# Row norms inverted as a 128x4 tile, masked logits in one combined pass with two exponentials, and a new issue order

## The chip, the cores and the metric

The kernel runs on one core of one Trainium2 chip, in float32. The metric is device microseconds of one execution, and lower is better. The time before is 2535.09 us, the median of three runs (2533.92 to 2537.39).

A core has TensorE (PE, matrix products and transposes), VectorE (DVE), ScalarE (ACT), GpSimd (POOL) and SyncE (SP). In this kernel SP issues nearly all DMAs, in one queue. PE writes its results to PSUM; all else lives in SBUF, 128 partitions wide.

## The reference

The input x has 32 batches of 512 tokens with 256 features, and one 512 x 512 adjacency (a 64th of it set) serves all batches. Per batch:

```python
def gat(inp, adj, W, a):                    # graph attention
    h = inp @ W
    f1, f2 = h @ a[:F, 0], h @ a[F:, 0]     # one number per token each
    e = leaky_relu(f1[:, None] + f2[None, :], 0.2)
    if adj is not None:
        e = where(adj > 0, e, -9e15)
    return elu(softmax(e, axis=-1) @ h)

y = layernorm(x)
o0 = relu(y @ mlp1_w + mlp1_b)                       # 512 x 512
o1 = elu(gat(o0, None, W_fc, a_fc)) + o0
o2 = relu(o1 @ mlp2_w + mlp2_b)                      # 512 x 256
x = x + relu(elu(gat(o2, adj, W_hand, a_hand)) + o2)

z = layernorm(x)                                     # slice attention, 8 heads of 64
fx, xm = z @ W_fx + b_fx, z @ W_x + b_x
w = softmax((xm @ W_slice + b_slice) / temp)         # token x 64 slices, per head
norm = w.sum(tokens)                                 # 8 heads x 64 slices = 512 numbers
tok = (w.T @ fx) / (norm + 1e-5)                     # 64 slice tokens per head
q, k, v = tok @ W_q, tok @ W_k, tok @ W_v
out = softmax(q @ k.T / 8) @ v
x = x + (w @ out) @ W_out + b_out
```

## The kernel before, in words

**Recording and issue order.** The program doesn't issue its instructions as it goes through the batches. A `Recorder` (line 52) records every operation of all 32 batches under its batch and under a step name: load, norm1, mlp1, h, factors, p, pv, o1, mlp2, h2, e, p2, pv2, norm2, w, sums, s1T, tokens, att, vo, gg, out. Then `order` (line 251) runs a list scheduler, `_schedule` (line 163), over them: it keeps a modelled time per engine, takes the operation that can start first, and among those that could start, the one with the smallest key. The key is the batch's number times a period plus the step's turn (`TURNS`, line 17; `PERIOD`, 23). A first pass over batches 1 to 12 measures the period, and the second pass takes each step's turn from where that step began in batch 8, with shifts by hand for the first three batches (`HEAD`) and the last three (`TAIL`). Costs of operations come from `_cost` (line 128) and the constants beside it: `SWITCH` is what PE loses between matmuls on different parts of the array, and `ISSUE, BEGIN, LAND, BEHIND` describe DMAs. At most four batches are interleaved. Finally `emit` (line 286) issues everything in that fixed order. So each engine has one fixed queue for the whole run, semaphores hold it to the data, and a change of a modelled cost can move every instruction of every engine. Nearly every instruction carries line 288, where `emit` issues it.

**The steps around the change.** In the middle batches (all but the first and the last) five big transposes and one small one go by DMA: DVE flips blocks of 32 x 32 into a staging tile (`flip`), four DMAs, one for each 32 partitions, write it to DRAM (`scr`), and one DMA reads it back transposed (`gather`). The tiles are xn_stage (first layernorm's result, read back as xnT for mlp1), u_stage (o1T), e_stage (p2T, the masked attention's weights for pv2), o2_stage (r2), xn2_stage (xn_raw, copied to xn2T for the weff products) and w_stage (w_raw, copied to wT for the out step). The first and the last batch transpose on PE, except o2.

- *norm1, mlp1*: DVE makes xn; xnT times w1 gives o0T on PE.
- *h*: o0T times W_fc in seven products of halves (Strassen and Winograd's way); DVE sums the left operands into `mix`.
- *pv, o1, mlp2, h2*: the attention without mask needs no 512 x 512 logits: its weights pT are built from vectors of 512. PE then does pT times h, the second layer and o2 times W_hand, with f1 and f2 as extra columns.
- *e*: four tiles of 128 rows. For each, DVE makes the logits (f2 from PSUM, f1 per row, `mbias` the mask as a large negative number), the leaky relu and the negated row maximum, ACT the exponential with that maximum as bias, and DVE the flip:

```python
nc.vector.scalar_tensor_tensor(
    e, f2b, h[:, i, D : D + 1], mbias[:, i, :], op0=OP.add, op1=OP.add)
nc.vector.scalar_tensor_tensor(e, e, ALPHA, e, op0=OP.mult, op1=OP.max)
nc.vector.tensor_reduce(nmax[:, i : i + 1], e, axis=AX.X, op=OP.max, negate=True)
nc.scalar.activation(e, e, AF.Exp, bias=nmax[:, i : i + 1])
```

- *norm2, w*: the second layernorm; xn2T times weff (W_x and W_slice in one) on PE, and its softmax over 64 slices per head on DVE and ACT.
- *sums*: xn times w, summed over tokens, into s1T (128 x 2 x 512). The last row of xn is 1, so s1T's last row holds the 512 norms.
- *s1T*: SP copies that one row to DRAM (`line`), and two DMAs spread it over the partitions of `rn` (128 x 256), where DVE adds 1e-5 and takes the reciprocal.
- *tokens, att, vo, gg*: W_fx times s1T (PE), times rn (DVE) is tok; then wqk times tok gives q, q times tok the scores, a softmax (sc, on DVE and ACT), its transposes and products with tokT (mean), and wvo to gg, one after another and each small.
- *out*: gg times wT on PE, added to x on DVE, and the store.

Of the kernel before, what the change touches and what calls it, by code (L numbers as in the profile page):

```python
# [10 lines left out]
AF = mybir.ActivationFunctionType  # L11
OP = mybir.AluOpType
AX = mybir.AxisListType
# [1 line left out]
ENGINES = ("tensor", "vector", "scalar", "gpsimd", "sync")  # L15

TURNS = {
    "load": -462.5, "norm1": 57.6, "mlp1": 1478.5, "h": 1624.1, "factors": 1626.7, "p": 1631.1,
    "pv": 1644.1, "o1": 1647, "mlp2": 1694.9, "h2": 1709.3, "e": 1714.6, "p2": 1102.3,
    "pv2": 1733.3, "norm2": 1780.6, "w": 1806.7, "sums": 1812.1, "s1T": 1826.8, "tokens": 2321.2,  # L20
    "att": 658.3, "vo": 1004.5, "gg": 1394.8, "out": 1524.2,
}
PERIOD, SPARE = 89.9, 0.01

HEAD = (
    (-33, 108, 3, -726, 0, 63, -4, 93, -317, -118, -101, -31, 114, 36, 581, -77, -43, -443, 55,
     -1, 16, -659),
    (302, 200, 0, 41, 0, 223, 198, 0, -15, 0, 760, -14, -1674, -151, 33, -31, -61, -1067, 191,
     -140, -300, 8),
    (-6, 37, 1179, -81, 0, 0, -1864, -1, 0, 1, -105, -68, -395, 94, 4, -151, 5, 3, -336, 3, 0,  # L30
     0),
)
TAIL = (
    (-203, -62, 1108, 0, -19, -60, 101, 4, -242, -90, -82, 1, -58, -418, -434, 1119, -43, -15,
     -10, 0, -198, 0),
    (295, 0, 75, 221, 12, 158, -7, 50, -1, 64, 0, 173, -8, -61, -5, 0, 30, 0, -59, -299, 730,
     197),
    (94, 1079, -126, 0, -154, 915, -18, 0, 0, -1924, -62, -58, -41, 72, -15, 360, 0, -238, 0,
     -132, -14, 140),
)  # L40


# [3 lines left out]

P = 128
ALPHA = 0.2
MASKED = -4.5e16


class Recorder:
# [3 lines left out]
    SIGNAL = 0.06  # L56
    DRAIN = 0.17
    ISSUE, BEGIN, LAND, BEHIND = 0.45, 2.2, 0.0, 3.6
    SWITCH = 0.1
    KEPT = 1  # L60
    AHEAD = 3

# [65 lines left out]
    def _cost(self, op, out, ins):  # L128


        def words(ap):
            return ap.size() // ap.ap[0][1]

        n = words(out)
        if op.method == "dma_start":
            side = next(ap for ap in (out, *ins) if ap.space != bass.MemoryType.DRAM)
            kb = out.size() / 256
            if side.ap[0][1] <= P // 4:
                op.moving = 0.3 + max(0.0, 1.08 * (kb / 128 - 1))
            else:  # L140
                op.moving = max(1.5 * kb / 512, 4.0 * kb / 1024 - 0.5)
            return self.ISSUE, 0.0
        if op.engine == "tensor":
            one = max(n / 1200 + 0.002, 0.109)
            if op.mode == (P, P // 2):
                one = max(n / 2400, 0.0275)
            elif op.mode == (P // 2, P // 2):
                one = max(n / 4800, 0.0135)
            return (one if op.method == "transpose" else 2 * one), self.DRAIN
        if op.engine == "scalar":  # L150
            pointers = sum(isinstance(op.kwargs.get(k), bass.AP) for k in ("bias", "scale"))
            return 0.06 + n / 1200 + 0.09 * pointers + 0.19 * ("accum_out" in op.kwargs), 0.12
        if op.engine == "vector":
            n = max([n] + [words(x) for x in ins])
            single = op.method in ("tensor_copy", "tensor_scalar")
            fast = single and all(x.space != bass.MemoryType.PSUM for x in ins)
            pointers = sum(words(x) == 1 for x in ins) if n > 1 else 0
            return 0.07 + n / (1920 if fast else 960) + 0.065 * pointers, 0.1
        if n < 16:
            return (0.1 if op.method == "memset" else 0.3 if op.method == "tensor_scalar" else 1.1), 0.1  # L160
        return 0.2 + n / (480 if op.method == "tensor_tensor" else 960), 0.1

    def _schedule(self, ops, key, spare):
# [35 lines left out]
        while len(done) < len(ops):  # L199
# [21 lines left out]
            if op.engine == "tensor" and op.mode != mode:  # L221
                t, mode = t + self.SWITCH, op.mode
            op.start, op.end = t, t + op.cost + op.lag
# [102 lines left out]
def adj_ffn_kernel(  # L326
# [26 lines left out]
    B, N, D = x.shape  # L353
    HID = mlp1_w.shape[1]
    HH = HID // 2
    NT = N // P
    KD = D // P
# [5 lines left out]
    NP = INNER // P  # L363
    assert G == C == 64 and HEADS * G == 512 and N == 512 and HID == 512 and D == 256

    nc = Recorder(tc.nc)
# [5 lines left out]
    def ts(i, n=P):  # L372
        return slice(i * n, (i + 1) * n)

    def new(name, shape, bufs=1, tag=None, dtype=F32):
        return sbuf.tile(list(shape), dtype, name=name, tag=tag or name, bufs=bufs)

    def mm_tile(shape):
        return psum.tile(shape, F32, tag="bank", name="mm", bufs=8)

    def tr_tile(shape):
        return psum.tile(shape, F32, tag="bank", name="tr", bufs=8)
# [7 lines left out]
    def flip(src, dst):  # L390

        nc.vector.transpose(dst, src.rearrange("p (c i) -> p c i", i=Q))

    def by_dma(what, b):

        return what in FLIPPED and b not in EDGES
# [19 lines left out]
    def med(name, shape=(P, 4, 256)):  # L416
        return new(name, shape, bufs=2, tag="med")

    def row(name, shape=(P, 512), tag=None):
        return new(name, shape, bufs=2, tag=tag)  # L420

    def small(name, shape):
        return new(name, shape, bufs=3)
# [8 lines left out]
    def load_x(b):  # L432
# [14 lines left out]
        out=ident, in_=ident, compare_op=OP.not_equal, fill=1.0, base=0,  # L447
# [75 lines left out]
    mbias = new("mbias", [P, NT, N], dtype=BF16)  # L523
# [10 lines left out]
    for t in range(NT):  # L534
# [4 lines left out]
        nc.vector.tensor_scalar(  # L539
            mbias[:, t, :], mbias[:, t, :], -1.0, -MASKED, op0=OP.add, op1=OP.mult  # L540
        )
# [69 lines left out]
    for p in range(NP):  # L611
        pv = mm_tile([P, D])
# [49 lines left out]
    def front(b):  # L662
# [20 lines left out]

        h = new("h", [P, NT, 2, HH + 1])
        l11, l12, l21, l22 = (o0T[:, ts(k, 2), ts(t, 2 * P)] for t in range(2) for k in range(2))
        mix = new("mix", [P, 4, 2, 2 * P])
        s1, s2, s3, s4 = (mix[:, i] for i in range(4))
        for to, left, op, right in (
            (s1, l21, OP.add, l22), (s2, s1, OP.subtract, l11),
# [32 lines left out]
        f1, f2 = h[:, :, 0, HH], h[:, :, 1, HH]  # L722
# [30 lines left out]
        pT = new("pT", [P, NT, N])  # L753
        for j in range(NT):
# [5 lines left out]
                op0=OP.mult, op1=OP.max,  # L760
# [6 lines left out]
        for i in range(NT):  # L767
# [9 lines left out]
            u, m = row("u"), row("m")  # L777
# [13 lines left out]
        if by_dma("u", b):  # L791
            gather("u", stage, o1T)
            for m in range(KH):
                o1 = o1T[:, m, :].rearrange("p (t a i) -> p t a i", t=NT, i=Q)
# [3 lines left out]
    def middle(b, o1T):  # L798
# [12 lines left out]
        h = new("h2", [P, NT, D + 2], tag="h" if b == B - 1 else None)  # L811
# [7 lines left out]
        f2b = tr_tile([P, N])  # L819
        for j in range(NT):  # L820
            nc.tensor.transpose(f2b[:, ts(j)], h[:, j, D + 1 : D + 2].to_broadcast([P, P]), ident)
        if not by_dma("e", b):
            pt, f2b = f2b, new("f2b", [P, N], tag="acb")
            nc.scalar.copy(f2b, pt)
        nc.step = "e"
        pT = new("p2T", [P, NT, N], tag="pT" if b == B - 1 else None)
        if by_dma("e", b):
            stage = new("e_stage", [P, N // Q, P], bufs=2, tag="stage")
        nmax = small("nmax", [P, NT])
        for i in range(NT):  # L830
            e = new("e", [P, N], bufs=2)
            nc.vector.scalar_tensor_tensor(
                e, f2b, h[:, i, D : D + 1], mbias[:, i, :], op0=OP.add, op1=OP.add
            )
            nc.vector.scalar_tensor_tensor(e, e, ALPHA, e, op0=OP.mult, op1=OP.max)
            nc.vector.tensor_reduce(
                nmax[:, i : i + 1], e, axis=AX.X, op=OP.max, negate=True
            )
            nc.scalar.activation(e, e, AF.Exp, bias=nmax[:, i : i + 1])
            if by_dma("e", b):  # L840
                flip(e, stage[:, :, ts(i, Q)])
                continue
            pt = tr_tile([P, NT, P])
            for j in range(NT):
                nc.tensor.transpose(pt[:, j, :], e[:, ts(j)], ident)
            nc.scalar.copy(
                pT.rearrange("p j (t a i) -> p j t a i", t=NT, i=Q)[:, :, :, i, :],
                pt.rearrange("p j (t i) -> p j t i", i=Q),
            )
# [18 lines left out]
        for i2 in range(NT // 2):  # L868
            parts = []
            for s in range(2):  # L870
                i = 2 * i2 + s
# [8 lines left out]
            u, m = row("u2", (P, 2, D), "u"), row("m2", (P, 2, D), "m")  # L880
# [10 lines left out]
    def back(b, x1):  # L891
# [17 lines left out]
        w = new("w", [P, NT, INNER], tag="o0T" if b == B - 1 else None, bufs=1 + (b == B - 1))  # L909
# [34 lines left out]
        s1T = med("s1T", (P, KD, INNER))  # L944
# [8 lines left out]
        if by_dma("w", b):  # L953
            raw = new("w_raw", [P, NP, N], tag="w")
            gather("w", stage_w, raw)
            for p in range(NP):
                nc.scalar.copy(
                    wT[:, p, :].rearrange("p (t a i) -> p t a i", t=NT, i=Q), swapped(raw[:, p, :])
                )
        nc.step = "s1T"  # L960
        line = dram.tile([NP, 2, G], F32, name="line", tag="line", bufs=2)
        nc.sync.dma_start(
            line.rearrange("(o p) s g -> o (p s g)", o=1), s1T[P - 1 : P, KD - 1, :]
        )
        rn = new("rn", [P, NP, G], tag="mean")
        for s in range(2):
            nc.sync.dma_start(
# [3 lines left out]
                    ap=[[0, C], [2 * G, NP], [1, G]],  # L971
                ),
            )
        nc.vector.tensor_scalar(rn, rn, 1e-5, None, op0=OP.add)
        nc.vector.reciprocal(rn, rn)
        nc.step = "tokens"

        nc.joint = True
# [17 lines left out]
        q = new("q", [P, 2, 2, G])  # L996
# [57 lines left out]
        gg = med("gg")  # L1054
# [33 lines left out]
    for b in range(B):  # L1088
        nc.age = b
        back(b, middle(b, front(b)))  # L1090
# [57 lines left out]
```

## Time and profile before

| | before |
|---|---|
| median of 3 runs | 2535.09 us (2533.92 to 2537.39) |
| the profiled execution, its own time | 2531.39 us |
| its span in the profile | 2529.6 us |
| mean granted TensorE clock | 0.996 |
| PE busy, matmuls | 2487.6 us |
| DVE busy | 2157.7 us |
| ACT busy | 1059.7 us |
| DMA moved | 348.60 MB |

The profiler recorded one execution. Its own time is 1.8 us longer than the span, and 3.7 us shorter than the median. Busy time is the sum over an engine's instructions, each from start to end. Matmuls overlap, so one starts before the other ends, and their mean durations are longer than the pitch at which they start. The chain of work that ended last is followed back from the last instruction, at each step to what released it. In lists of instructions, a line reads: line of the code, engine, operation, output<-inputs by the program's names, shapes, count; idle time before, with what ended it, stands in brackets or behind the last bar.

### The profile page before, as it was taken

To read this page: it belongs to the slowest core of one execution; us is meant where nothing else is said; L and a number is where in the kernel's file an instruction comes from. 1 tells how busy PE (TensorE), PEld (TensorE's weight loads), DVE (VectorE), ACT (ScalarE), POOL (GpSimd) and SP (SyncE) were. 2 spreads that over 40 slices of the span, in tenths; PEclk is the share of its full clock that TensorE was granted. 3 is DMA by queue.
4 is the path that set the end of the run, shared out by engine and by line. 5 is a ranking of instruction groups with operands and counts; after the bars stand their busy time and mean duration, and the time that the engine had idled before them with its cause. 6 is when DMAs were issued, how large, how long until landed. Compare 5 with 4: busy or idle time off the path is not lost.

```text
span 2529.6 us, 33819 instructions
## 1 busy us (share of the span) xinstructions
PE 2487.6 (98%) x11653; PEld 1726.1 (68%) x11653; DVE 2157.7 (85%) x5108; ACT 1059.7 (42%) x1941; POOL 101.1 (4%) x167
## 2 busy tenths in 40 slices
PE   7999999999999999999999999999999999999988
PEld 5767667776667666677666676766676666767655
DVE  7778889988889888889888898888898888888865
ACT  3434343433444434444434434334444344444432
POOL 0000000000000000000000000000000000000000
PEclk9999999999999999999999999999999999999989
DMA  5243456544556544555544565445565445545432
GB/s 162 59 120 94 130 155 169 158 128 127 136 160 170 148 126 131 151 160 160 135 132 128 160 172 148 131 134 136 160 169 144 127 130 155 162 127 148 109 97 63
DMA packets 441985, 348.60 MB, mean 138 GB/s; under 512 B 101044, under 2 KB 366388, under 8 KB 441814
## 3 DMA queue, kind: packets, MB, share of 16 engines
q1 hardware_dynamic: 440230, 345.39, 50.3%
q8 instruction: 93, 1.52, 0.2%
q10 hardware_dynamic: 1584, 1.05, 0.1%
q14 instruction: 78, 0.64, 0.1%
HBM read 186.92 MB, written 159.45 MB: 137 GB/s over the span
## 4 chain that ended last, share of the span: by engine, by line
PE 81%; ACT 6%; DVE 6%; DMA 5%; SPq 1%; issue 1%; POOL 0%; DVEq 0%; ACTq 0%
PE mm L288 79%; ACT pT L288 2%; PE tr L288 2%; DMA rn<-line 2%; ACT acb L288 2%; SPq L288 1%; DMA xn_raw<-scr 1%; ACT o2T L288 1%; DVE rn L288 1%; DVE acb L288 1%; DMA scr<-xn_stage 1%; DVE u L288 1%; DVE h L288 1%; DVE xn_stage L288 1%; DVE xn L288 0%
## 5 line engine op out<-in xcount | busy, mean ns | idle before, releaser
L288 PEld LDWEIGHTS mm<-h,pT 128*128 128x128 f32 x2048 | 385.8, 189 | 152.0 <-issue 87.9
L288 PE MATMUL mm<-h,pT 128*128 128x257 f32 (+1 forms) x2048 | 483.8, 379 | 1.6 <-DVE pT L288 1.6
L288 PE MATMUL mm<-weff,xn2T 128*128 128x512 f32 x512 | 256.3, 607 | 1.7 <-ACT xn2T L288 1.7
L288 PE MATMUL mm<-w,xn 128*128 128x512 f32 x512 | 252.8, 592 | 0.0
L288 PE MATMUL mm<-o1T,w 128*128 128x512 f32 x512 | 246.8, 593 | 0.8 <-DVE o1T L288 0.8
L288 PE MATMUL mm<-xnT,w 128*128 128x512 f32 x512 | 232.3, 603 | 0.7 <-ACT xnT L288 0.7
L288 PE MATMUL mm<-gg,wT 128*128 128x256 f32 x1024 | 230.5, 379 | 0.8 <-DVE gg L288 0.8
L288 PE MATMUL mm<-h,p2T 128*128 128x257 f32 x1024 | 228.2, 380 | 0.0
L288 PEld LDWEIGHTS mm<-gg,wT 128*128 128x128 f32 x1024 | 193.6, 190 | 41.0 <-issue 15.0
L288 ACT ACTIVATE e<-e,nmax 128x512 f32<-128x512 f32 x128 | 92.4, 722 | 294.9 <-DVE nmax L288 294.8
L288 PEld LDWEIGHTS mm<-h,p2T 128*128 128x128 f32 x1024 | 194.0, 190 | 29.4 <-issue 1.2
L288 DVE TENSOR_TENSOR h<-mm,h 128x257 f32<-128x257 f32 x320 | 128.8, 419 | 61.7 <-PE mm L288 61.0
L288 PEld LDWEIGHTS mm<-xnT,w 128*128 128x128 f32 x512 | 95.1, 191 | 107.9 <-issue 102.5
L288 ACT ACTIVATE m<-m 128x512 f32<-128x512 f32 x192 | 120.9, 630 | 112.2 <-DVE m L288 112.2
L288 ACT COPY h<-mm 128x258 f32<-128x258 f32 (+1 forms) x256 | 95.0, 373 | 135.9 <-PE mm L288 135.3
L288 ACT ACTIVATE u<-mm,rd 128x256 f32<-128x256 f32 x192 | 90.3, 470 | 145.0 <-DVE rd L288 68.4
L288 ACT ACTIVATE w<-w 128x512 f32<-128x512 f32 x128 | 80.7, 630 | 162.4 <-DVE w L288 162.2
L288 DVE SCALAR_TENSOR_TENSOR pT<-acb,ex,pT 128x512 f32<-128x512 f32 x128 | 94.0, 745 | 63.8 <-ACT pT L288 63.8
L288 ACT ACTIVATE m<-m,neg 128x512 f32<-128x512 f32 x192 | 138.4, 721 | 5.3
L288 DVE SCALAR_TENSOR_TENSOR u<-m,u 128x512 f32<-128x512 f32 x192 | 129.7, 675 | 11.7 <-ACT m L288 11.5
L288 ACT COPY xn2T<-xn_raw 128x512 f32<-128x512 f32 x60 | 34.2, 615 | 245.9 <-DMA xn_raw<-scr 245.9
L288 PEld LDWEIGHTS mm<-o1T,w 128*128 128x128 f32 x512 | 91.6, 189 | 58.0 <-issue 39.5
(150 smaller groups left out, 4208.8 us busy)
## 6 DMA issues: line engine op xcount, KB each, us to landing
scr<-xn_stage SPq DMA_DIRECT2D x240, 128.0 KB, 2.5
scr<-u_stage SPq DMA_DIRECT2D x120, 256.0 KB, 5.9
o1T<-scr SPq DMA_DIRECT2D x30, 1024.0 KB
scr<-e_stage SPq DMA_DIRECT2D x120, 256.0 KB, 4.9
p2T<-scr SPq DMA_DIRECT2D x30, 1024.0 KB, 5.5
scr<-w_stage SPq DMA_DIRECT2D x120, 256.0 KB, 4.8
w_raw<-scr SPq DMA_DIRECT2D x30, 1024.0 KB, 7.9
x<-in_x_dram SPq DMA_DIRECT2D x32, 512.0 KB
```

The lines of the kernel that those rows point to most:

```text
L288: getattr(getattr(self.nc, op.engine), op.method)(*op.args, **op.kwargs)
```

## The change

- The planner: all of `TURNS`, `PERIOD`, `HEAD` and `TAIL` are new; `SWITCH` goes from 0.1 to 0.17, the modelled cost of a 64 x 64 matmul up by a fifth, and `reciprocal` gets a cost of its own.
- `mix` shares the buffer of `pT`.
- e: one `tensor_tensor_reduce` per tile adds f2 and the mask and takes the row maximum (`top`) in the same instruction; the profile's program has it as two, the pass and a read of its 128x1 result. f1, being one number per row, is added to the four maxima at once (128 x 4), which then go through the leaky relu. The leaky relu of the logits is left to ACT: exp of a maximum is the maximum of exponentials, so ACT takes one exponential with f1 - top as bias and one of 0.2 times the logit, and DVE takes the larger. Four tiles e are held instead of two, since all four maxima come before the first exponential. `MASKED` is a power of two.
- s1T: the norms' row goes by DMA into a tile of 128 x 4 (`norm`), is inverted there, goes to DRAM and is then spread; `rn` arrives inverted. That is one DMA per batch more.

```diff
@@ TURNS, PERIOD, HEAD, TAIL: all numbers
-    "load": -462.5, "norm1": 57.6, "mlp1": 1478.5, "h": 1624.1, "factors": 1626.7, "p": 1631.1,
...
-PERIOD, SPARE = 89.9, 0.01
+    "load": 361.5, "norm1": -64.6, "mlp1": 945.4, "h": 1108, "factors": 1115.3, "p": 1133,
...
+PERIOD, SPARE = 89.08, 0.01
...
-MASKED = -4.5e16
+MASKED = -(2.0 ** 55)
...
-    SWITCH = 0.1
+    SWITCH = 0.17
...
-                one = max(n / 4800, 0.0135)
+                one = max(n / 4000, 0.0135)
...
+            if op.method == "reciprocal":
+                return 0.05 + n / 145, 0.1
...
-        mix = new("mix", [P, 4, 2, 2 * P])
+        mix = new("mix", [P, 4, 2, 2 * P], tag="pT")
...
-        nmax = small("nmax", [P, NT])
-        for i in range(NT):
-            e = new("e", [P, N], bufs=2)
-            nc.vector.scalar_tensor_tensor(
-                e, f2b, h[:, i, D : D + 1], mbias[:, i, :], op0=OP.add, op1=OP.add
-            )
-            nc.vector.scalar_tensor_tensor(e, e, ALPHA, e, op0=OP.mult, op1=OP.max)
-            nc.vector.tensor_reduce(
-                nmax[:, i : i + 1], e, axis=AX.X, op=OP.max, negate=True
-            )
-            nc.scalar.activation(e, e, AF.Exp, bias=nmax[:, i : i + 1])
+        f1, top, low = h[:, :, D], small("top", [P, NT]), small("low", [P, NT])
+        masked = [new("e", [P, N], bufs=4) for i in range(NT)]
+        for i, e in enumerate(masked):
+            nc.vector.tensor_tensor_reduce(
+                out=e, in0=f2b, in1=mbias[:, i, :], scale=1.0, scalar=3.0 * MASKED,
+                op0=OP.add, op1=OP.max, accum_out=top[:, i : i + 1],
+            )
+        nc.vector.tensor_tensor(top, top, f1, op=OP.add)
+        nc.vector.scalar_tensor_tensor(top, top, ALPHA, top, op0=OP.mult, op1=OP.max)
+        nc.vector.scalar_tensor_tensor(low, f1, ALPHA, top, op0=OP.mult, op1=OP.subtract)
+        nc.vector.tensor_tensor(top, f1, top, op=OP.subtract)
+        for i, e in enumerate(masked):
+            above = row("above", tag="m")
+            nc.scalar.activation(above, e, AF.Exp, bias=top[:, i : i + 1])
+            nc.scalar.activation(e, e, AF.Exp, scale=ALPHA, bias=low[:, i : i + 1])
+            nc.vector.tensor_tensor(e, e, above, op=OP.max)
             if by_dma("e", b):
                 flip(e, stage[:, :, ts(i, Q)])
...
         nc.step = "s1T"
+        norm = new("norm", [P, NP], bufs=2)
+        nc.sync.dma_start(norm, s1T[P - 1 : P, KD - 1, :])
+        nc.vector.tensor_scalar(norm, norm, 1e-5, None, op0=OP.add)
+        nc.vector.reciprocal(norm, norm)
         line = dram.tile([NP, 2, G], F32, name="line", tag="line", bufs=2)
-        nc.sync.dma_start(
-            line.rearrange("(o p) s g -> o (p s g)", o=1), s1T[P - 1 : P, KD - 1, :]
-        )
+        nc.sync.dma_start(line.rearrange("p s (q f) -> (p s q) f", f=NP), norm)
         rn = new("rn", [P, NP, G], tag="mean")
...
-        nc.vector.tensor_scalar(rn, rn, 1e-5, None, op0=OP.add)
-        nc.vector.reciprocal(rn, rn)
```

## The prediction

> **What bounds the kernel now.** First the page: busy times, then the chain of work that ended last.
>
> ```profile
> span 2529.6 us, 33819 instructions
> PE 2487.6 (98%) x11653; PEld 1726.1 (68%) x11653; DVE 2157.7 (85%) x5108; ACT 1059.7 (42%) x1941; POOL 101.1 (4%) x167
> ...
> PE 81%; ACT 6%; DVE 6%; DMA 5%; SPq 1%; issue 1%; POOL 0%; DVEq 0%; ACTq 0%
> ```
>
> TensorE is on 81% of the chain. Its 98% alone would not prove it the bound, since overlapped matmuls inflate it; so I took stretches next (columns: time in the stretch, busy of PE, weight load, DVE, ACT, POOL, granted clock, DMA share, GB/s).
>
> ```profile
> 1000.00:1080.00 80.00, 79.88 (x376) 56.13 (x376) 70.67 (x166) 33.20 (x61) 3.19 (x5) 1.00 0.52 140
> 2380.00:2440.00 60.00, 52.72 (x296) 37.02 (x297) 42.42 (x95) 24.46 (x46) 1.32 (x3) 0.93 0.48 124
> 2440.00:2500.00 60.00, 55.68 (x268) 34.18 (x261) 48.04 (x102) 25.07 (x47) 1.37 (x3) 0.95 0.28 73
> ```
>
> In the middle PE has 0.12 us idle of 80; in the last 150 us it has holes. PE's idle sums to 42 us: about 14 before 60 us, 19 after 2380, 9 in the 2300 between. A batch's mark on the chain (its first pT) recurs every 76.7 to 78.0 us, on average 76.9. Counting that period's matmuls by the pitch at which they start (64 of 512 columns at 0.4285, 200 of 256 to 258 at 0.2162, 5.1 us of small ones) gives 75.7, so 1.2 us a batch are hand-overs to and from PE. **A change that adds no matmul (6104 before and after, apart from repeats in the records) can win at most about 1.2 us a batch, and what the two ends hold.** The ends, on PE's timeline (bracket: idle before it and releaser):
>
> ```profile
> 2432.02 1.17 PE L288 MATMUL mm<-tok,wqk 128*128 128x256 f32 x2 [2.81 <-DVE tok L288]
> ...
> 2437.39 0.69 PE L288 MATMUL tr<-ident,sc 128*128 128x128 f32 x2 [2.42 <-DVE sc L288]
> ...
> 2441.53 3.78 PE L288 MATMUL mm<-weff,xn2T 128*128 128x512 f32 x4
> 2488.48 0.70 PE L288 MATMUL mm<-tok,wqk 128*128 128x256 f32 x2 [2.06 <-DVE tok L288]
> ```
>
> Batch 29's token chain (tokens, wqk, att, wvo) runs with nothing between its links.
>
> **What the Trainium skill says.** "TensorE: Matmul & The Clock Gate", Part 1: PE idle for about 3.4 us falls to half clock. The trace agrees: after 2428 to 2439, mostly idle, four weff matmuls took 3.78 us, against 1.88 for four alike at 2424.65. "VectorE: DVE Perf Modes", Walkthrough: reciprocal is an iterative divide; below, 1751 ns against 294 for an addition on the same tile. The same page (Two Vector instructions): an accumulating operation issues a second instruction that reads the sum; the trace has 84 ns for it. "DMA: Bandwidth & Descriptors", Anatomy: about 2.0 us fixed per DMA; here line<-s1T was issued at 2501.80 and rn<-line, which needs it, at 2503.94.
>
> **Part 1, row norms.** Groups kept apart by shape (busy, mean ns | idle before):
>
> ```profile
> L288 DVE TENSOR_REDUCE nmax<-e 128x1 f32<-128x512 f32 x128 | 87.0, 681 | 0.0
> L288 DVE SCALAR_TENSOR_TENSOR e<-tr,h,mbias 128x512 f32<-128x512 f32 x120 | 86.2, 739 | 3.8 <-PE tr L288 3.8
> L288 DVE SCALAR_TENSOR_TENSOR e<-e 128x512 f32<-128x512 f32 x128 | 84.2, 678 | 0.0
> L288 DVE RECIPROCAL rn<-rn 128x256 f32<-128x256 f32 x32 | 56.0, 1751 | 0.9
> L288 DVE TENSOR_SCALAR rn<-rn 128x256 f32<-128x256 f32 x32 | 9.4, 294 | 21.7 <-DMA rn<-line 21.5
> ...
> L288 DVE RECIPROCAL ra<-ra 128x4 f32<-128x4 f32 x32 | 5.5, 171 | 0.1
> L288 DVE DVE_READ_ACCUMULATOR m<-wfc,ab 128x1 f32 x8 | 0.7, 84 | 0.0
> L288 ACT ACTIVATE e<-e,nmax 128x512 f32<-128x512 f32 x128 | 92.4, 722 | 294.9 <-DVE nmax L288 294.8
> ```
>
> Removed: 1.75 + 0.29 = 2.05 us. Added: a 128x4 addition (0.22, as ex) and reciprocal (0.17): **-1.65 us of DVE**. One DMA is added per batch (32 in all), of 16-byte rows: one SP issue of about 0.7 us (median of line's; it goes up to 1.3) and a hop of about 2.1. The waits it adds: on SP norm<-s1T waits for the s1T copy, and xn_stage, xnT and line are queued behind it (part 3); on DVE the addition waits for norm to land, with two u_stage flips behind it, and stands some 4 us of operations behind the xn_stage flips (at S + 7 in part 3's clock, norm issued at S + 1.5 and 2.0 to land), so it waits for nothing: 0. line waits for the reciprocal, with w_raw, rn and u_stage behind it on SP; tok stands 46 operations (some 25 us) behind that reciprocal, line's 2.1 and rn's 5.6 fit in that: 0 in the middle.
>
> **Part 2, masked logits.** Removed on DVE, a batch: 4 x (0.739 + 0.678 + 0.681) = 8.39. Added: four combined passes, four 128x4 operations (0.9), four maxima (0.685). The combined pass is not in this trace. Low end 0.74 + 0.08, as the scalar_tensor_tensor that reads the same operands; high end 1.4, two passes. I take the low end, since it too reads two operands and writes one: 6.94, **-1.45 us of DVE**; with the high end +1.2. ACT: four more exponentials, **+2.9 us** on 33 of 77: free in the middle, where nothing on the chain is behind them. The row maxima now need all four logits ahead of the first exponential; the four e buffers allow it. By the issue order, DVE spans 16.3 to 17.4 us from first logit to last flip, with 33.2 us from its start to pv2 (before 32.3). With the e DMAs (4.9 and 5.5) 2.7 us are left, as now (2.6): **0** in the middle.
>
> So DVE goes from about 67.4 to 64.3 us a batch. PE doesn't wait for the average, so this alone gives little: **0 to -1.2 us a batch**.
>
> **Part 3, new turns.** I walked the new order batch by batch. What moves nearest to PE's needs is the first layernorm's transposition. Before (timeline; bracket absent: no wait):
>
> ```profile
> 944.31 2.69 SPq L288 DMA_DIRECT2D scr<-xn_stage  x4
> ...
> 949.62 0.97 SPq L288 DMA_DIRECT2D xnT<-scr  x1
> ...
> 956.27 4.13 PE L288 MATMUL mm<-xnT,w 128*128 128x512 f32 x9
> ```
>
> The sums matmuls end at S = 943.7; the last xn_stage flip ends at S + 0.5, xnT lands (3.6 to 5.1) about 1.5 us before mlp1 wants it at S + 12.55. After, three more DVE passes precede the last flip (S + 2.45), and norm, which waits for s1T, stands before xn_stage in SP's queue: xnT at S + 7.9, landed at S + 11.4 to 13.1. Stall 0 to 0.6; I take **0.1**. On norm2's way the flips follow three o1T additions; xn2T meets weff within 0.5 us: 0.1 to 0.4, before 0.5 with o2T. The other hand-overs (wh to f's transposes, q, attT, wvo) stay; my sum of these waits is 1.4 after against 1.5: **-0.1 us a batch (-0.6 to +0.5), -3 over 27 batches**. mix now shares pT's one buffer: its first addition waits for the batch before to finish pv (long done at S + 13, PE stands at mlp1), and pT's first write waits for the last product of h, on which it depends anyhow through f1 and f2: 0.
>
> **Ends.** Tail, batch 29: between its wqk, att and wvo now lie w2 (6.9 us) and h2 of the last batch; of 7.2 us of waits and 3 of slow clock I count 8 saved. Batch 30's rn is covered by eight weff matmuls: 2 of the 4.2 us that DVE lost there. The last batch's e step, formerly spread over four tiles, now needs eight exponentials (5.8 us of ACT) after all four passes, with less PE work around it: +4. Its pv2 comes earlier by less work in front: -1.8. The last norm: a hop more (2.1 + 0.5) against 0.3 + 1.75: +0.6. Sum **-7 (-12 to -2)**. Head: DVE has eight operations more (2.8 us) before batch 0's pT, but stands less behind the x loads: **+1 (0 to +2)**.
>
> Sum: -3 - 7 + 1 = -9 on the profiled execution of 2531.4. That lies 3.7 below the median of the runs shown, so I set -9 to -11 against 2535.1: **2524.5**.
>
> **Rivals.**
> - *DVE's relief lets PE's hand-overs close*: 1.2 x 27 = -32, with the tail 2495. For it: 70.67 of 80 us of DVE are busy, its queue in order. Against: most hand-overs are single dependences of 0.2 to 0.5 us that a free DVE doesn't shorten. 0.12.
> - *Nothing*: e and norm were hidden, and the ends only trade waits: 2533. 0.10.
> - *Slower by xnT*: the norm issue ahead of xn_stage holds SP until s1T; if xnT's issue-to-landing is over 4.7 us, mlp1 waits in every batch. At 0.6 us x 28 = +17 with the ends' -6: 2546. For it: p2T, of double size, already lands in 5.5. Against: xnT landed in time throughout. It decides from a flip end later than S + 2. 0.18.
> - *Slower by the combined pass*: if it takes 1.4 us, DVE gains 2.3 us in the stretch from e to xn_stage, where nothing is spare, and everything behind, xnT first, is late by about as much: +2.3 x 28 = 2592. 0.10.
>
> **How the numbers follow.** The forecast case has 0.50, its own range 2512 to 2537. Differences of 0.2%, 5 us, are about what a measurement of this kernel can tell: 2530 and 2540 bound "same". Faster: 0.37 of the forecast case, 0.12, 0.02 of "nothing" = 0.51. Same: 0.10 + 0.07 + 0.03 (of xnT) = 0.20. Slower: 0.03 + 0.01 + 0.15 + 0.10 = 0.29. The range 2502 to 2555 leaves out most of the first and of the last rival.
>
> **What would show it.** Right: DVE's busy sum falls by about 95 us (3.1 x 32), ACT's rises by 92; the mark's period is 76.5 to 77; PE's idle after 2380 falls below 14 us. Wrong: a combined pass over 0.9 us; mlp1's first matmul with over 0.5 us <-ACT xnT per batch; PE waiting for p2T in the middle.

## The result, and the profile after

The changed kernel takes 2548.18 us (median of 6 runs, 2540.91 to 2549.65), beside 2533.85 us for the kernel before on the same occasion: a ratio of 1.0049 (95% interval 1.0037 to 1.0061). By the ratio it is slower by half a per cent, 12 us (the medians lie 14 us apart), where 0.4% faster was forecast. On two later occasions, on two different chips, the same pair gave 1.0018 (1.0010 to 1.0027) and 1.0054 (1.0042 to 1.0066). Slower it is each time, but by how much differs. The profiled execution took 2548.94 us, its span is 17.6 us longer than that of before.

The page of the kernel after, its busy times and its chain:

```profile
span 2547.2 us, 34086 instructions
PE 2493.8 (98%) x11653; PEld 1722.5 (68%) x11653; DVE 2041.9 (80%) x5236; ACT 1095.2 (43%) x2069; POOL 95.0 (4%) x167
...
PE 59%; DVE 20%; DMA 12%; ACT 6%; issue 2%; SPq 1%; POOL 0%; DVEq 0%; ACTq 0%
```

DVE gave back 116 us of work, and yet PE's share of the chain fell from 81% to 59%: what the chain passes through instead are DVE and DMA. The same three stretches as before (columns as in the prediction):

```profile
1000.00:1080.00 80.00, 78.41 (x366) 53.53 (x365) 65.02 (x168) 34.69 (x66) 3.00 (x5) 1.00 0.54 143
2380.00:2440.00 60.00, 59.81 (x273) 41.18 (x272) 47.74 (x123) 25.93 (x48) 0.57 (x3) 1.00 0.44 112
2440.00:2500.00 60.00, 57.38 (x316) 37.40 (x315) 42.21 (x104) 28.28 (x53) 2.13 (x4) 1.00 0.36 102
```

The end has filled up as forecast (0.19 us idle where there were 7.28), and the middle, which had 0.12 us idle of 80, has 1.59. An engine's busy time in a stretch counts overlapping instructions once (it isn't the sum over its instructions: ACT's groups after add up to 1183.5 us, the page has 1095.2), so PE's idle time is the stretch less its busy time. It went from 13.9 to 19.8 us in the first 60 us, from 9.4 to 20.8 between 60 and 2380, and from 18.6 to 12.4 behind 2380; as these cuts are fixed times, the two kernels don't do quite the same work between them. That is 11 of the 17.6 us; the other 6 lie in PE's busy time. The granted clock was 0.86 instead of 0.94 in the first 60 us, which may be a part of it; how much is not shown.

For the middle I use one mark per batch, PE's transpose of fm, and take the 22 periods from batch 7 to 29. Their mean is 76.99 us before and 77.65 us after (+14.5 us over the 22). The shortest is 76.69 in both. So the shortest period did not move; more batches miss it. The waits that tell why, as "engine waited for: us in total, times, longest" between 500 and 2210 us. ACT in the kernel before:

```profile
ACT wT L288 <- DMA w_raw<-scr: 3.1, 5, 1.4
```

ACT in the kernel after:

```profile
ACT wT L289 <- DMA w_raw<-scr: 18.6, 18, 1.8
```

PE in the kernel after (before, it had no wait of either kind in this stretch):

```profile
PE mm L289 <- DMA xnT<-scr: 5.4, 5, 2.7
PE mm L289 <- ACT xn2T L289: 4.3, 4, 1.6
```

Before, the wT copies stood on ACT behind the u and m operations of the attention without mask, and beside the first h copies:

```profile
1187.51 0.72 ACT L288 ACTIVATE m<-m,neg 128x512 f32<-128x512 f32 x1
...
1192.69 1.13 ACT L288 COPY wT<-w_raw 128x512 f32<-128x512 f32 x2
```

After, they stand ahead of a u and two m (ACT's timeline under "Repairs" below).

SP's timeline and then PE's show one late xnT:

```profile
1343.98 3.11 SPq L289 DMA_DIRECT2D scr<-xn_stage  x4
...
1350.70 0.38 SPq L289 DMA_DIRECT2D xnT<-scr  x1
```

```profile
1348.08 5.81 PE L289 MATMUL mm<-h,p2T 128*128 128x257 f32 x26
1356.61 7.09 PE L289 MATMUL mm<-xnT,w 128*128 128x512 f32 x12 [2.72 <-DMA xnT<-scr]
```

Before, mlp1 started 6.6 us after xnT's issue (949.62 and 956.27), 1.5 us more than its median landing of 5.1. In this batch of the kernel after, PE is done with the 26 products at 1348.08 + 26 x 0.2162 = 1353.7, 3.0 us after the issue, while xnT's median landing is 3.8 us. Over the middle batches mlp1 started 6.2 to 7.5 us after xnT's issue before, and 3.7 to 5.9 us after. Little time is left in hand, and PE stopped for xnT in 5 of the 22.

The head, on DVE and on PE:

```profile
26.27 0.68 DVE L289 TENSOR_TENSOR mix<-o0T 128x512 f32<-128x512 f32 x1
29.19 1.29 DVE L289 TENSOR_TENSOR wfx<-wfx,m 128x512 f32<-128x512 f32 x2 [2.24 <-DMA m<-in_L_ffn_W_fx_dram]
...
31.67 0.68 DVE L289 TENSOR_TENSOR mix<-mix,o0T 128x512 f32<-128x512 f32 x1
```

```profile
27.00 3.79 PE L289 MATMUL mm<-mixed,mix 128*128 128x257 f32 x8 [4.77 <-DVE mix L289]
...
52.38 7.99 PE L289 MATMUL mm<-h,pT 128*128 128x257 f32 x26 [4.04 <-DVE pT L289]
```

Batch 0's mix stands behind set-up work that waits for the W_fx load, so the first pT product comes at 52.38. Before, it came at 46.53:

```profile
46.53 10.22 PE L288 MATMUL mm<-h,pT 128*128 128x257 f32 x46 [1.62 <-DVE pT L288]
```

Last, DVE's groups that are new:

```profile
L289 DVE TENSOR_TENSOR e<-e,above 128x512 f32<-128x512 f32 x128 | 82.3, 679 | 3.6 <-ACT e L289 3.6
L289 DVE CUSTOM_DVE_ANT_0 e<-tr,mbias 128x512 f32<-128x512 f32 x120 | 81.5, 682 | 3.3 <-PE tr L289 3.3
...
L289 DVE DVE_READ_ACCUMULATOR2_ANT top<- 128x1 f32 x128 | 10.7, 83 | 0.0
...
L289 DVE TENSOR_SCALAR norm<-norm 128x4 f32<-128x4 f32 x32 | 5.3, 165 | 8.7 <-DMA norm<-s1T 8.6
```

The arithmetic costs about what it was priced at: the combined pass 0.68 us and 0.083 for its read, and each of the exponentials on ACT 0.71 us (0.72 before). The loss is elsewhere.

### The profile page after: what moved, and what is told of

It is laid out like the page before. It is cut to its first block, busy times and chain, and to the rows that moved or that the text cites. A ratio compares the mean times of both kernels' runs of the same rounds, so it can differ in the third digit from the quotient of the medians.

```text
span 2547.2 us, 34086 instructions
## 1 busy us (share of the span) xinstructions
PE 2493.8 (98%) x11653; PEld 1722.5 (68%) x11653; DVE 2041.9 (80%) x5236; ACT 1095.2 (43%) x2069; POOL 95.0 (4%) x167
## 4 chain that ended last, share of the span: by engine, by line
PE 59%; DVE 20%; DMA 12%; ACT 6%; issue 2%; SPq 1%; POOL 0%; DVEq 0%; ACTq 0%
PE mm L289 57%; DMA scr<-w_stage 4%; DMA w_raw<-scr 3%; DVE e L289 3%; DVE w L289 3%; PE tr L289 2%; DVE rs L289 2%; DVE w_stage L289 2%; DVE e_stage L289 1%; DVE pT L289 1%; ACT acb L289 1%; DMA scr<-xn_stage 1%; DMA xn_raw<-scr 1%; DVE mx L289 1%; DVE x L289 1%
## 5 line engine op out<-in xcount | busy, mean ns | idle before, releaser
L289 PE MATMUL mm<-h,pT 128*128 128x257 f32 (+1 forms) x2048 | 466.3, 380 | 4.0 <-DVE pT L289 4.0
L289 PE MATMUL mm<-o1T,w 128*128 128x512 f32 x512 | 241.3, 596 | 0.0
L289 PE MATMUL mm<-w,xn 128*128 128x512 f32 x512 | 239.7, 593 | 0.2 <-DVE w L289 0.2
L289 PE MATMUL mm<-gg,wT 128*128 128x256 f32 x1024 | 237.9, 382 | 0.8 <-DVE gg L289 0.8
L289 ACT COPY q<-mm 128x256 f32<-128x256 f32 x32 | 11.9, 371 | 370.3 <-PE mm L289 370.3
L289 DVE SCALAR_TENSOR_TENSOR u<-m,u 128x512 f32<-128x512 f32 x192 | 130.8, 682 | 34.9 <-ACT m L289 34.0
L289 PEld LDWEIGHTS mm<-w,xn 128*128 128x128 f32 x512 | 93.1, 189 | 76.6 <-issue 59.8
L289 ACT COPY h<-mm 128x257 f32<-128x257 f32 (+1 forms) x256 | 92.7, 371 | 111.2 <-PE mm L289 110.8
L289 PE MATMUL mm<-wfc,mix 128*128 128x257 f32 x512 | 137.6, 385 | 0.0
```

Source lines behind the costliest of these rows:

```text
L289: getattr(getattr(self.nc, op.engine), op.method)(*op.args, **op.kwargs)
```

## The experiments

The planner makes the issue order anew for every edit, so that a plain edit changes all four queues at once. Most kernels below therefore keep the order of the changed kernel and alter single operations, or the place of a few, where `emit` issues them; apart from what is named, the orders of PE, DVE, ACT and SP are equal. All ratios are to the kernel before on the same occasion, with 95% intervals; each of the four occasions was on another chip. The first (e1 to e4) had no run of the unaltered changed kernel, so its gains are counted from c1, the changed kernel on the second, at 1.0018. On the third it had 1.0054 (c2), and from there each of these gains would be 9 us larger: they are rough. "The hop" below is the added way of the norms: the DMA norm<-s1T, DVE's two operations on norm, and line<-norm behind them.

**Head (e1).** One number:

```diff
 HEAD = (
-    (0, -29, 160, 21, 3, -112, ...
+    (0, -29, 160, -726, 3, -112, ...
```

> The changed kernel with one number of HEAD changed: the shift of batch 0's step h goes from 21 back to -726. The issue order differs only in the first 60 us: batch 0's mix additions stand on DVE ahead of the wfx and wx set-up products, which wait for the W_fx load. Theory (the head's loss is a queue effect: mix stood behind a late load): the first pT matmul comes at about 46 to 47 us instead of 52.4, and the time falls by 4 to 6 us, to about 2543. Rival (the head is bound by the loads as a whole, and DVE only waits elsewhere): no change beyond 2 us.

Measured: 2527.66 us, 0.9992 (0.9983 to 1.0000). PE's timeline:

```profile
45.53 7.63 PE L289 MATMUL mm<-h,pT 128*128 128x257 f32 x34 [1.61 <-DVE pT L289]
```

The first pT product came 6.9 us earlier than in the changed kernel's first profile (c1 had it at 50.23, c2 at 51.50). Counted from c1 the gain is 0.26%, 6.6 us. The clean test is e9 against e8 below, which differ by this one number and ran side by side: 8.5 us. The head's loss is the place of mix in DVE's queue, as the theory had it.

**Waits of PE taken away (e2, e3).** The order is kept; the operand changes:

```diff
-    pm, w1[:, k, ts(m)], xnT[:, k, :], ...
+    pm, w1[:, k, ts(m)], w1[:, k, :], ...        # e2 and e3
-    pm, xnT[:, k, ts(t)], weff[:, k, :], ...
+    pm, weff[:, k, ts(t)], weff[:, k, :], ...    # e3 only
```

> The changed kernel in exactly its own issue order on every engine, but in batches 1 to 30 mlp1 multiplies by w1 in place of xnT, so PE waits for no xnT (xnT is still flipped, written and read back; the values of the output change). Theory X (the new turns leave no time between xnT's issue and mlp1, so that each late landing stops PE): the middle's period falls from 77.67 towards 77.1, the time by 8 to 14 us to 2534 to 2540. Rival N (the extra norm hop delays u_stage and what follows it): less than 4 us. Rival Z (the stop only moves to the next hand-over, xn2T): 2 to 6 us, and the waits for xn2T grow.

> As the kernel before it in this list (mlp1 reads w1 in place of xnT), and the weff products of batches 1 to 30 also read weff in place of xn2T: PE waits for neither transposed layernorm. Theory X with xn2T as the second late tile: the period reaches about 76.7, the period of the kernel before, and the time falls by 13 to 18 us, to about 2531 to 2535. If the middle's loss has another cause (norm's hop, the exponentials on ACT), the period stays above 77.2 and the time falls by less than 10 us.

Measured: e2 2533.67 us, 1.0008 (1.0001 to 1.0015); e3 2531.32 us, 0.9999 (0.9991 to 1.0007). Counted from c1 that is 2.5 and 4.8 us, less than theory X wanted for either; counted from c2 it would be 11.6 and 13.9, as theory X had it. So the gain of freeing xnT alone is not settled, and e2 and e3 overlap. What stands without a control is the period, from one profile each: 77.23 us in e2, and 76.97 in e3, that of before, so PE's two waits do carry the middle's loss in the end. Why xn2T is late lies upstream.

**Without the hop (e4).**

```diff
-        nc.sync.dma_start(norm, s1T[P - 1 : P, KD - 1, :])
-        nc.vector.tensor_scalar(norm, norm, 1e-5, None, op0=OP.add)
+        nc.vector.tensor_scalar(norm, mhalf, 1e-5, None, op0=OP.add)
...
-        nc.sync.dma_start(line.rearrange("p s (q f) -> (p s q) f", f=NP), norm)
+        nc.sync.dma_start(line.rearrange("p s (q f) -> (p s q) f", f=NP), s1T[P - 1 : P, KD - 1, :])
```

> The changed kernel in its own issue order, but in batches 1 to 30 the DMA norm<-s1T is left out, the 128x4 operations read a constant, and line takes s1T's row directly (so tok is scaled by the norms, not by their inverses). It takes away the added DMA, SP's wait for s1T ahead of xn_stage and DVE's wait for norm. Theory X (turns): xnT stays as late as it is, less than 3 us gained. Rival N (the hop): DVE's waits for norm (0.6 us in the late batches) and SP's place ahead of xn_stage go, 8 to 16 us gained, the period near 76.9.

Measured: 2529.64 us, 0.9991 (0.9982 to 0.9999), 6.8 us counted from c1, period 77.02. From the lower of the two controls this is between the two theories, and speaks against the first: the hop is not free.

**Control, ACT's wait, mlp1 later, old turns (c1, e5, e6, e7).** For these I had followed the chain of the changed kernel back from a late xn2T: w_stage's DMAs, w_raw's read-back, three wT copies on ACT, and behind them in ACT's queue o0T, u and m, on which DVE's o1T and the second layernorm wait. e5 tests that, again in the same order:

```diff
-    nc.scalar.copy(wT[:, p, :]..., swapped(raw[:, p, :]))
+    nc.scalar.copy(wT[:, p, :]..., swapped(weff[:, p % KD, :]))
```

> The changed kernel unaltered, as the control: the kernels compared with it so far ran at another time than it did. Theory L (with no slack left between DMA landings and their readers, its time moves with how fast the DMAs happen to land): well below 2548, 2532 to 2540, and its waits for xnT and xn2T sum to less than 9.7 us. Rival (the loss is a fixed one of the order): again 2544 to 2549, so that e1's one number in HEAD was worth about 20 us.

> The changed kernel in its own issue order, but in batches 1 to 30 ACT's four copies to wT read weff in place of w_raw, so that they wait for no read-back (the values of the output change). In the changed kernel ACT waited for w_raw in 18 of 22 middle batches, with o0T, u and m of other steps queued behind it. Theory W (this wait at the head of ACT's queue makes xn2T late): the waits for xn2T go, and the time falls by 3 to 6 us against the control of this list. Theory X (only xnT counts): less than 2 us.

> The changed kernel with the head's repair (mix ahead of wfx and wx) and one move on PE: from batch 6 to 29, the last three pv2 matmuls of another batch go ahead of mlp1's first six instead of behind them, so that mlp1 wants xnT some 1.3 us later; DVE, ACT and SP keep their orders. Theory X: xnT then lands in time, the middle's period comes to 76.8 to 76.9 and the time to 2518 to 2526, below the kernel before. Rival (mlp1's delay moves to o0T and mix on DVE, 1.3 us a batch at worst): 2530 to 2550.

> The new arithmetic and cost constants with TURNS, PERIOD, HEAD and TAIL of the kernel before. If the new turns are what costs time (theory T), the old ones on the new arithmetic give 2515 to 2535. Rival (turns fit only the arithmetic that they were made for): the xn flips fall some 10 us behind the last w operation on DVE in this order, against 4.5 in the changed kernel, mlp1 waits in every batch, and the time rises by 20 to 100 us.

Measured: c1 2536.18 us, 1.0018 (1.0010 to 1.0027), with waits for xnT and xn2T of 6.9 us, which speaks for theory L in this comparison. e5 2529.88 us, 0.9994 (0.9985 to 1.0002): 6 us below c1, its neighbour, period 76.96 against 77.37. PE's waits for xn2T fell from 4.1 to 1.2 us. Theory W holds, at the upper end of its figure. e6 2534.78 us, 1.0014 (1.0007 to 1.0020): it is 0.22% slower than e1, of the occasion before, whose order it has but for the move. PE's wait for xnT is gone from its list, but the shortest period rose from 76.69 to 77.08, and DVE's waits for ACT's u grew (58.0 us against 38.8 in c1). The rival was right: this delay of mlp1 is passed on. e7 2820.22 us, 1.1145 (1.1125 to 1.1165), with PE waiting mainly for pT:

```profile
PE mm L290 <- DVE pT L290: 89.0, 27, 4.2
```

Turns fit only the operations for which they were set. Taking the arithmetic alone, with the old turns, is no test of the arithmetic. The size was missed (20 to 100 us expected, 289 measured), and so was the place: PE waited for pT, not for xnT in every batch.

**Repairs (c2, e8, e9, e10).** ACT's timeline in the first control (c1) shows where the copies could stand:

```profile
1354.98 1.66 ACT L289 COPY wT<-w_raw 128x512 f32<-128x512 f32 x3
1356.55 0.68 ACT L289 ACTIVATE o0T<-mm,b 128x512 f32<-128x512 f32 x1
1357.13 0.60 ACT L289 COPY wT<-w_raw 128x512 f32<-128x512 f32 x1
...
1364.25 0.37 ACT L289 COPY h<-mm 128x257 f32<-128x257 f32 x1 [0.49 <-PE mm L289]
1378.47 0.37 ACT L289 COPY q<-mm 128x256 f32<-128x256 f32 x1 [13.85 <-PE mm L289]
```

Behind the wT copies ACT's queue holds u and m (at 1357.64 and 1358.60), on which DVE waits. After the h copies ACT has nothing to do for 13.9 us, and wT is first read at 1392. e8 moves the four copies there; e9 has e8's move and e1's number, and leaves nothing out; e10 is e9 without the hop, as e4.

```diff
 order of ACT, batches 4 to 27
-o0T o0T wT wT wT o0T wT u m o0T m h h h h
+o0T o0T o0T u m o0T m h h h h wT wT wT wT
```

> The changed kernel once more, as the control beside the three that follow. Theory L (its time hangs on DMA landings): 2533 to 2549, slower than the kernel before by 0.1 to 0.5%. Rival (the first control was the odd one): 2545 to 2549 again.

> The changed kernel with one move on ACT in batches 4 to 27: the four wT copies, which wait for w_raw, go behind the four h copies that followed them, where ACT sat idle for 13.9 us (seen in the first control); the other engines keep their orders and nothing is left out. gg times wT comes some 25 us later. Theory W (the wait for w_raw at the head of ACT's queue costs the middle): ACT's waits for w_raw fall from 18 us to under 5, PE's for xn2T from 4 to under 2, the time by 4 to 8 us against the control. Rival X (only xnT's own lateness counts): less than 2 us.

> Both moves: batch 0's mix ahead of wfx and wx (one number of HEAD), and the wT copies behind the h copies on ACT. The arithmetic is that of the changed kernel. If head and wT are the two queue effects that cost the time, they add: 10 to 14 us below the control, 2522 to 2526, and 5 to 9 us below the kernel before (a ratio of 0.9965 to 0.998). If xnT alone holds the middle, it stays within 3 us of e1.

> The repaired kernel without the added DMA: in batches 1 to 30 norm<-s1T is left out, the 128x4 operations read a constant and line takes s1T's row (tok is scaled by the norms, not by their inverses). Theory: with wT out of the way the hop is covered, less than 2 us. Rival N (the hop itself delays xn_stage or u_stage): 4 to 7 us more gained.

Measured, on one occasion: c2 2549.49 us, 1.0054 (1.0042 to 1.0066), just above both ranges, and so rather the rival's. e8 2536.66, 1.0007 (0.9999 to 1.0014), 12.8 us below the control, more than the 4 to 8 expected. e9 2528.15, 0.9975 (0.9967 to 0.9982), 8.5 us further. e10 2519.93, 0.9942 (0.9930 to 0.9954), 8.2 us further still, so that its theory (the hop is covered) was wrong. In e8 ACT's wait for w_raw is gone from its list, and PE's for xn2T fell from 4.1 to 1.7 us. DVE's wait for ACT's u, which stood behind the copies, shows the way on; in c2

```profile
DVE m L289 <- ACT u L289: 39.4, 44, 2.4
```

and in e8

```profile
DVE m L304 <- ACT u L304: 17.9, 45, 0.5
```

Head and copies add up, to 21.3 us below the control, more than the 10 to 14 expected; the ratio to the kernel before is in the expected range. The changed arithmetic, so placed, is faster than the kernel before.

**What of the hop costs (e11 to e14).** The edit of e11 is e10's with the norm DMA issued all the same; e12 moves the DMA and what follows from it:

```diff
 order of SP, batches 4 to 27
-norm xn_stage w_stage xnT line w_raw rn u_stage o1T
+xn_stage w_stage xnT norm w_raw u_stage line rn o1T
```

> The repaired kernel with the DMA norm<-s1T in its place, but in batches 1 to 30 nothing reads what it brings: the 128x4 operations read a constant and line takes s1T's row (tok is scaled by the norms). If the hop's 8 us are DMA traffic or SP's place ahead of xn_stage, this is as slow as the repaired kernel (0.9965 to 0.998 of the kernel before). If they are DVE's wait for norm, with u_stage's flips behind it, and line's wait for the reciprocal, with w_raw and u_stage behind it on SP, it is as fast as without the hop (0.993 to 0.9955).

> The repaired kernel, whole arithmetic, with norm's steps moved in batches 4 to 27: on SP norm<-s1T goes behind xnT, line and rn behind u_stage's four DMAs; on DVE the addition and the reciprocal go behind the last u_stage flip. If only the hop's place was wrong, 0.993 to 0.9955 of the kernel before, and no wait of DVE for norm. If the DMA itself costs, 0.9965 to 0.998.

> The repaired kernel once more, as the control beside the other three: 0.9967 to 0.9982 of the kernel before, as in its first run, if the ratio does not depend on the occasion; the unaltered changed kernel's did (1.0018 to 1.0054).

> The repaired kernel without the added DMA once more (batches 1 to 30: norm<-s1T left out, the 128x4 operations read a constant, line takes s1T's row, so tok is scaled by the norms): 0.993 to 0.9955 if the hop's 8 us are real, within 0.1% of the repaired kernel if they were chance.

Measured: e13 2521.90 us, 0.9961 (0.9949 to 0.9974); e14 2517.80, 0.9947 (0.9935 to 0.9960); e11 2518.86, 0.9949 (0.9935 to 0.9962); e12 2524.25, 0.9972 (0.9961 to 0.9983). The repaired kernel beats the kernel before a second time, by 0.4%. The hop came to 3.5 us here, with intervals that overlap, after 8.2 us the time before. e11 stands with e14, which would point to what waits for norm and away from the traffic, but its interval overlaps the repaired kernel's. Nor does it free all that waits: DVE's addition overwrites the tile that the DMA fills, and still waited for it (5.4 us in e11, 0.4 of them between 500 and 2210). What e11 does take away is line's dependence on the reciprocal. SP then waits less for line's landing, which rn and then u_stage's DMAs stand behind; in e13 and e11, between 500 and 2210:

```profile
SPq L304 <- DMA line<-norm: 57.2, 22, 3.5
SPq L309 <- DMA line<-s1T: 29.9, 22, 1.7
```

The same wait is 60.6 to 65.0 us in the unaltered changed kernel, 61.8 in e9 and 67.7 in e12, and 30.3 to 34.9 in e4, e10 and e14, which have no hop. It is the likeliest way by which the hop delays the rest, but no run tests it by itself. e12 was no better than the repaired kernel, so the place that I chose is no cure: norm landed sooner (3.6 us, 5.6 in e13), but o1T's read-back now stood behind line and rn, and DVE waited 6.8 us for it and PE 3.8 for DVE's o1T. How the hop costs its 3 to 8 us stays open.

## Why the prediction was wrong

**Sign and size.** The forecast was 9 to 11 us faster; the change made the kernel 12 us slower by the ratio (0.0049 x 2534). The measured 2548.18 us lies inside the range of 2502 to 2555, in the part that was left to the rivals.

**Right.** The combined pass at the low end; DVE's relief (95 us forecast, 116 measured); no matmul added, and a best period that did not move. The tail: -7 forecast, PE's idle behind 2380 fell by 6.2 us, to 12.4. The exponentials cost no wait of PE for p2T beyond 0.7 us over the whole run. ACT's busy time rose by 35.5 us, not by the 92 named as a sign: the exponentials themselves grew from 92.4 to 170.2 us, and the page's total counts the overlap of two that follow each other once.

**Wrong: "-0.1 us a batch".** This is the step that failed. I summed PE's hand-overs after at 1.4 us against 1.5, from walks along PE's and DVE's orders. ACT's order I had walked for the exponentials only. There the wT copies had moved to just before w_raw lands, ahead of u and m; the waits for w_raw went from 3.1 to 18.6 us, and e5 and e8, each against a control beside it, priced their effect at 6 and 12.8 us. The measured term, with all that delayed the middle, is +0.66 us a batch, +14.5 over 22.

**Half right: xnT.** The rival "slower by xnT" gave 2546, close to the time, and its point (flips later than S + 2) held: in the batch shown above the sums ended at about 1341.2 and the last xn_stage flip at 1344.0. But it had 0.6 us in each of 28 batches. In the trace it was 5.4 us over five batches, 0.25 us a batch, where I had put 0.1. The 3.6 to 5.1 us that I had read for xnT's landing before are its shortest and its median; the longest was 6.8, so the spread was larger than I allowed for. What taking the wait away brings (e2) is not settled. So it was by chance that its time came out close: the wT copies, the head and the hop are the larger effects.

**Wrong: the hop at 0 in the middle.** I took 2.0 to 2.1 us for it from line's issue at the empty end of the run. In the middle, where large transfers are under way, its two DMAs took:

```profile
norm<-s1T SPq DMA_DIRECT2D x22, 2.0 KB, 6.1
line<-norm SPq DMA_DIRECT2D x21, 2.0 KB, 4.3
```

So DVE did wait for norm, 8.6 us in the whole run and 2.5 of them between 500 and 2210, and the hop was worth 8.2 us on one occasion and 3.5, not clear of noise, on another.

**Wrong: the head at +1.** I counted DVE's added operations and the x loads, and missed that mix had gone behind wfx and wx, which wait for a load: PE's idle rose by 5.9 us, and e9 took 8.5 us back against e8.

## What to carry to other kernels

When a plan moves instructions, walk every queue, not only those of the bounding engine and of the busiest: a copy that is cheap, on an engine with time to spare, delays what stands behind it once it waits for a DMA (here 6 to 13 us of 2540). Judge a hand-over by the time it has in hand against the spread of landings in the busy stretch, not by the median, nor by a landing taken where the queues are empty. And price arithmetic and order apart: here the new arithmetic in the new order, with two places mended, was worth -0.25 to -0.4%, and those two places turned it into +0.2 to +0.5%.

## What the hardware showed that I had not expected

A DMA of 2 KB (norm<-s1T) took 6.1 us to land in the busy middle, longer than one of 512 KB on the same queue (xnT, 3.8 us). Behind 2380 the median of its three landings was 2.0 us. The place in the queue counts too: moved behind xnT (e12), it landed in 3.6 us in the middle. The Trainium skill ("DMA: Bandwidth & Descriptors", Anatomy of one DMA) gives a fixed cost of about 2.0 us for a DMA that GpSimd issues. SP issues the ones here; that median at the end agrees with the figure, and the middle does not.

PE's clock fell to half without an idle stretch as long as the 3.4 us that the prediction cites. In its lines the two wqk products at 2432.02 took 1.17 us, against 0.70 at 2488.48; the idle stretch ahead of them was 2.81 us, the longest between 2410 and the four slow weff products, with small matmuls on either side.

The changed kernel's ratio moved by 0.36% between occasions (1.0018 and 1.0054), with separate intervals, while the medians of the kernel before lay within 2531.3 to 2534.6 us on all five. An order without time in hand may read out how DMAs happen to land; this is argued from its waits, and no run varied the landings by themselves. As the two occasions were on different chips, a difference between chips is an open rival, and nothing here tells them apart.
